# Layer 0 of a graph-then-attention kernel: two product reads placed between the left sums, and a fixed order for the opening

## The chip, the cores and the metric

The kernel runs on one core of one Trainium2 chip. The metric is the device time of one execution in microseconds (us); the figure for a kernel is the median of its runs. The core has a matrix engine (TensorE, "PE" in the profile; its weight loads are listed apart as "PEld"), a vector engine (VectorE, "DVE"), an activation engine (ScalarE, "ACT"), a general engine (GpSimd, "POOL"), and a queue that issues the transfers (SyncE, "SP"). SBUF is the memory beside the engines, and PSUM the small memory in banks into which TensorE writes. Each engine runs its own list of instructions in order, and waits on semaphores for what other engines produce.

## The reference: what is computed

There are 64 batch elements of 256 nodes with 512 features, and one graph over the 256 nodes. Layer 0 mixes along the graph, layer 1 is masked attention with 8 heads; each ends in a residual addition and a normalization over the features.

```python
a = adj.astype(x.dtype)
deg = a.sum(axis=1)
# layer 0
mi = x @ Wi.T                      # Wi, Wj: the two halves of W
mj = x @ Wj.T
x = layernorm(x + deg * (mi + b) + a @ mj)
# layer 1: q, k, v = x @ W.T + bias, softmax over the neighbours only
# ... (cut)
x = layernorm(x + attn_out @ Wo.T + bo)
```

## The kernel before: the parts concerned

The kernel handles the batch in 32 groups of two elements, b1 and b2. Every block product is done as seven products of half size instead of eight (a scheme of the Strassen-Winograd kind): the left operand is split into blocks A11, A12, A21, A22, of which sums S1 to S4 are formed, and the right operand (the weights) into blocks and sums B11, B21, B22, T1 to T4. VectorE forms the left sums. In layer 0 the left operand is the input multiplied by the graph. The input is split first into a rounded part `xhi` and a remainder `xlo`, and the graph product of both parts lands in a PSUM bank `pa` for each of four chunks of 128 features.

A tile that is drawn from `bank(...)` takes the next of three PSUM banks in rotation. It can be written only when all readers of the tile that had this bank before are done.

```python
ps_m = ctx.enter_context(tc.tile_pool(name="ps_m", bufs=3, space=PSUM))
def bank(name):
    return ps_m.tile([P, 512], F32, tag="mm", name=name)
def in_order(ins):                      # the scheduler keeps the program's order for these
    tc.keep_in_program_order(ins)
def anywhere(ins):                      # the scheduler may move these on their engine
    pass
# ... (cut)
for n, w, j in ((B11, wiT, 0), (T3, wiT, 1), (B22, wjT, 1), (B21, wjT, 0)):
    nc.sync.dma_start(out=w0[:, n], in_=...)
    if n == B11:
        nc.sync.dma_start(out=b_bc, in_=b0.to_broadcast([P, D]))
load_x(1)
# ... (cut)
for t in range(NT):                     # the graph, transposed
    pt = bank("pt_a")[:, :N]
    # ... transposes into pt
    nc.vector.tensor_copy(graph[:, t, edges(t)], pt)
    nc.scalar.copy(aT[:, t, :], pt)
# ... (cut)
def split_x(b):
    in_order(nc.scalar.copy(xhi[b], xh[b]))
    in_order(nc.gpsimd.tensor_tensor(xlo[b], xh[b], xhi[b].bitcast(F32), ALU.subtract))
    if b == 0:
        degree_bias()                   # two tensor_scalar of 128x512 on VectorE
    in_order(nc.gpsimd.tensor_tensor(xh[b], xh[b], degb, ALU.add))
# ... (cut)
def combine_left(f, order=anywhere):
    nc.vector.tensor_add(f["S1"], f["A21"], f["A22"])
    nc.vector.tensor_sub(f["S2"], f["S1"], f["A11"])
    order(nc.vector.tensor_sub(f["S3"], f["A11"], f["A21"]))
    nc.vector.tensor_sub(f["S4"], f["A12"], f["S2"])
def take_input(b, c, pa):               # the same for one chunk of layer 0, from PSUM
    nc.scalar.copy(xl[b][:, c]..., pa[:, :3 * P])
    _, a12, a22, a21 = (pa[:, m * P:(m + 1) * P] for m in range(4))
    f = xS[b]
    nc.vector.tensor_add(f["S1"][:, c], a21, f["A22"][:, c])
    nc.vector.tensor_sub(f["S3"][:, c], f["A11"][:, c], a21)
    nc.vector.tensor_sub(f["S2"][:, c], a22, f["S3"][:, c])
    nc.vector.tensor_sub(f["S4"][:, c], a12, f["S2"][:, c])
def first_inputs(b):                    # only for the first element
    pas = [score_banks("pa")[:, 0, :] if c < 2 else bank("pa") for c in range(NC)]
    for k, part in enumerate((xhi[b], xlo[b])):
        for c in range(NC):
            # ... graph products of chunk c into pas[c]
            if k == 1:
                take_input(b, c, pas[c])
```

The seven products of layer 0 run in the order below; the products 3, 6 and 7 accumulate onto the banks of 1, 4 and 5 ("x", "y", "z"), so those must have been read first.

```python
def l0_steps(b):
    def add_to(dst, src):
        nc.vector.tensor_add(dst, src, dst)
    # step1: A11*B11 -> x, copied to u1 by ScalarE; GpSimd adds u1 to three quarters of xh
    # step2: A22*T4 -> w      step3: A12*B21 onto x
    def step4():
        product("y", "S2", T2, True)
        add_to(place(0, 1), banks["y"])
    def step5():
        product("z", "S1", T1, True)
        add_to(place(1, 1), banks["z"])
    # step6: S3*T3 onto y, add_to, norm of row half 1
    # step7: S4*B22 onto z, add_to, norm of row half 0
```

The opening, before the loop, and the last slot of each turn of the loop, in which the second element's steps 4 to 7 (`rest`) are mixed with the output projection of the group before (`o`):

```python
split_x(0)
for n, m, k in ((T1, T3, B11), (T2, B22, T1), (T4, B21, T2)):
    in_order(nc.vector.tensor_sub(w0s[n], w0s[m], w0s[k]))       # 128x1024 each
first_inputs(0)
in_order(nc.vector.tensor_sub(w0s[T3], w0s[B22], w0s[T3]))
p, q = l0_steps(0), l0_steps(1)
run([p[0], p[2], p[1]])
split_x(1)
run(p[3:5])
bias_steps()
make_factors(wqT, "wq", raw_q)          # four 128x512 subtractions on VectorE
run(p[5:])
l0_inputs(1, 0, ...); l0_inputs(1, 1)   # graph stage of the second element
make_factors(wkT, "wk", raw_k)
# ... (cut)
run(q[:2]); h_transpose(0, 1, True); run(q[2:3]); h_transpose(0, 0, True)
check_graph()
run(q[3:])
# ... (cut), then in the loop over 31 groups:
    inverses = divide_at_once(g, w + 1)   # two reciprocals, two multiplications on VectorE
    o = o_steps(g)
    rest = work[SLOTS]                    # steps 4 to 7 of layer 0, element b2
    run(o[:1] + rest[:1] + o[1:2] + rest[1:2])
    combine_left(oS[g], in_order)
    end_values(inverses)
    run(rest[2:] + o[2:5] + work[SLOTS + 1] + o[5:6] + work[SLOTS + 2] + o[6:])
```

Of the kernel before, what the change touches and what calls it, by code (L numbers as in the profile page):

```python
# [225 lines left out]
def unshifted_path(ctx, tc, flag, x, adj, wiT, wjT, b0, wqT, bq, wkT, bk, wvT, bv, woT, bo, out):  # L226
# [70 lines left out]
    def load_x(b):  # L297
        if b < B:
            xh[b] = p6.tile([P, NT, D], F32, tag="xh", name="xh")
            nc.sync.dma_start(out=xh[b], in_=x[b].rearrange("(t p) d -> p t d", p=P))  # L300
# [4 lines left out]

    for n, w, j in ((B11, wiT, 0), (T3, wiT, 1), (B22, wjT, 1), (B21, wjT, 0)):
        nc.sync.dma_start(out=w0[:, n], in_=w.rearrange("(c p) o -> p c o", p=P)[:, :, j * H:(j + 1) * H])
        if n == B11:
            nc.sync.dma_start(out=b_bc, in_=b0.to_broadcast([P, D]))
    load_x(1)  # L310


    ident = const.tile([P, P], F32, name="ident")
# [21 lines left out]
    def diagonal(t):  # L335
        return slice(2 * t * P, (2 * t + 1) * P)

    def edges(t):
        return slice((1 - t) * P, (3 - t) * P)
# [3 lines left out]
    for t in range(NT):  # L343
        pt = bank("pt_a")[:, :N]
        for i in range(NT):
            transpose(pt[:, i * P:(i + 1) * P], a[:, i, t * P:(t + 1) * P], ident)

        nc.vector.tensor_copy(graph[:, t, edges(t)], pt)
        nc.scalar.copy(aT[:, t, :], pt)

    inexact = const.tile([P, 1], F32, name="inexact")

    def check_graph():


        exact = p1.tile([P, NT, 3 * P], F32, tag="oS", name="exact")
        for t in range(NT):
            nc.vector.tensor_copy(exact[:, t, edges(t)], aT[:, t, :])
            nc.vector.tensor_scalar(exact[:, t, diagonal(t)], ident, deg[:, t:t + 1], None, ALU.mult)
        nc.vector.tensor_tensor(exact, exact, graph.bitcast(F32), ALU.not_equal)  # L360
        nc.vector.tensor_reduce(inexact, exact.rearrange("p t n -> p (t n)"), AX.X, ALU.max)
        nc.vector.tensor_scalar(maskT, aT, 0.0, MASK, ALU.is_equal, ALU.mult)

    def degree_bias():
        for t in range(NT):
            in_order(nc.vector.tensor_scalar(degb[:, t, :], b_bc, deg[:, t:t + 1], None, ALU.mult))

    xhi, xlo, xl, xS, hT, hS, qT, kT, vv, aoT, oS = ({} for _ in range(11))

    def split_x(b):  # L370

        if b < B:
            xhi[b] = p1.tile([P, NT, D], F32R, tag="xhi", name="xhi")
            in_order(nc.scalar.copy(xhi[b], xh[b]))
            xlo[b] = p1.tile([P, NT, D], F32R, tag="xlo", name="xlo")
            in_order(nc.gpsimd.tensor_tensor(xlo[b], xh[b], xhi[b].bitcast(F32), ALU.subtract))
            if b == 0:
                degree_bias()
            in_order(nc.gpsimd.tensor_tensor(xh[b], xh[b], degb, ALU.add))


    def load_bias(b, name):
# [82 lines left out]
        order(nc.scalar.activation(shift, below, AF.Identity, scale=rstd))  # L465
        order(nc.scalar.activation(t, t, AF.Identity, bias=shift, scale=rstd))  # L466

    def norm(t):
        norm_apply(t, *norm_stats(t))

    def left_blocks(a11, a12, a21, a22, s):
        return {"A11": a11, "A12": a12, "A21": a21, "A22": a22,
                "S1": s[:, 0], "S2": s[:, 1], "S3": s[:, 2], "S4": s[:, 3]}

    def combine_left(f, order=anywhere):
        nc.vector.tensor_add(f["S1"], f["A21"], f["A22"])
        nc.vector.tensor_sub(f["S2"], f["S1"], f["A11"])
        order(nc.vector.tensor_sub(f["S3"], f["A11"], f["A21"]))
        nc.vector.tensor_sub(f["S4"], f["A12"], f["S2"])


    def input_tiles(b):
# [28 lines left out]
    def first_inputs(b):  # L511

        input_tiles(b)
        pas = [score_banks("pa")[:, 0, :] if c < 2 else bank("pa") for c in range(NC)]
        for k, part in enumerate((xhi[b], xlo[b])):
            for c in range(NC):
                for t in range(NT):
                    graph_product(b, c, pas[c], k * NT + t, t, part)
                if k == 1:
                    take_input(b, c, pas[c])  # L520

    def l0_steps(b):
        banks = {}

        def product(name, lname, n, first):
            if first:
                banks[name] = bank("po")[:, :H]
            for c in range(NC):
                matmul(banks[name], xS[b][lname][:, c, :], w0[:, n, c, :], start=(first and c == 0),
                                 stop=(c == NC - 1), skip_group_check=True)  # L530

        def place(t, j):
            return xh[b][:, t, j * H:(j + 1) * H]

        def add_to(dst, src):
            nc.vector.tensor_add(dst, src, dst)  # L536

        def step1():
            product("x", "A11", B11, True)
            u1 = p2.tile([P, H], F32, tag="lu", name="u1")  # L540
            nc.scalar.copy(u1, banks["x"])

            rest = xh[b].rearrange("p t (j o) -> p (t j) o", j=2)[:, 1:]
            nc.gpsimd.tensor_tensor(rest, rest, u1.unsqueeze(1).to_broadcast([P, 3, H]), ALU.add)  # L544

        def step2():
            product("w", "A22", T4, True)
            add_to(place(1, 0), banks["w"])

        def step3():  # L550
            product("x", "A12", B21, False)
            add_to(place(0, 0), banks["x"])

        def step4():
            product("y", "S2", T2, True)
            add_to(place(0, 1), banks["y"])

        def step5():
            product("z", "S1", T1, True)
            add_to(place(1, 1), banks["z"])  # L560

        def step6():
            product("y", "S3", T3, False)
            h = xh[b][:, 1, :].rearrange("p (j o) -> p j o", j=2)
            add_to(h, banks["y"].unsqueeze(1).to_broadcast([P, 2, H]))
            norm(xh[b][:, 1, :])

        def step7():
            product("z", "S4", B22, False)
            add_to(place(0, 1), banks["z"])  # L570
            norm(xh[b][:, 0, :])

        return [step1, step2, step3, step4, step5, step6, step7]

    def h_transpose(b, t, borrow=False):

        g, i = divmod(b, NB)
        if i == 0 and t == 1:
            hT[g] = p1.tile([P, NC, NB * N], F32, tag="hT", name="hT")
            hS[g] = pair_blocks(hT[g], "hS")  # L580
        pt = (score_banks("pt_h")[:, 0, :] if borrow else bank("pt_h")).rearrange("p (c n) -> p c n", c=NC)
        for c in range(NC):
            transpose(pt[:, c, :], xh[b][:, t, c * P:(c + 1) * P], ident)
        nc.scalar.copy(hT[g][:, :, i * N + t * P:i * N + (t + 1) * P], pt)
        if t == 0 and i == NB - 1:
            combine_left(hS[g])

    def add_output_bias(b):

# [289 lines left out]
    raw_q, raw_k = load_raw(wqT, "kT"), load_raw(wkT, "oS")  # L879
    load_x(2)  # L880
    raw_v, raw_o = load_raw(wvT, "v"), load_raw(woT, "aoT")
    split_x(0)
    w0s = [w0[:, n] for n in range(7)]
    for n, m, k in ((T1, T3, B11), (T2, B22, T1), (T4, B21, T2)):
        in_order(nc.vector.tensor_sub(w0s[n], w0s[m], w0s[k]))
    first_inputs(0)
    in_order(nc.vector.tensor_sub(w0s[T3], w0s[B22], w0s[T3]))
    p, q = l0_steps(0), l0_steps(1)
    run([p[0], p[2], p[1]])
    split_x(1)  # L890
    run(p[3:5])
    bias_steps()
    make_factors(wqT, "wq", raw_q)
    run(p[5:])
    l0_inputs(1, 0, (score_bank, score_bank))
    l0_inputs(1, 1)
    make_factors(wkT, "wk", raw_k)
    for _ in range(AHEAD):
        bring()
    run(q[:2])  # L900
    h_transpose(0, 1, True)
    run(q[2:3])
    h_transpose(0, 0, True)
    check_graph()
    run(q[3:])
    q = qk_steps(0, qT, "qT", bq_sb, bqd)
    run(q[:1])
    fold_value_bias(raw_o)
# [16 lines left out]
    for g in range(NG - 1):  # L925
        load_x(NB * (g + 2))
        load_x(NB * (g + 2) + 1)
        work = layer0(g + 1)
        run(work[0])
        for w in range(2, NB * NC, 2):  # L930
            values(g, w - 2)
            values(g, w - 1)
            multiply()
            divide_two(g, w - 1)
            later = [scores(g, w), scores(g, w + 1)]
            part = work[w // 2]
            n = 0 if w == NB * NC - 2 else 1
            run(later[:n] + part[:1] + later[n:] + part[1:])
        w = NB * NC - 2
        values(g, w)  # L940
        values(g, w + 1)
        multiply()
        inverses = divide_at_once(g, w + 1)
        o = o_steps(g)
        rest = work[SLOTS]
        run(o[:1] + rest[:1] + o[1:2] + rest[1:2])
        combine_left(oS[g], in_order)
        end_values(inverses)
        run(rest[2:] + o[2:5] + work[SLOTS + 1] + o[5:6] + work[SLOTS + 2] + o[6:])
        end = finish_steps(g)  # L950
        q = qk_steps(g + 1, qT, "qT", bq_sb, bqd)
        k = with_output_bias(g + 1, qk_steps(g + 1, kT, "kT", bk_sb, bkd))
        v = v_steps(g + 1)
        run(q[:5] + end[:1] + q[5:6] + end[1:2] + q[6:7] + end[2:3] + k[:1] + end[3:4] + k[1:] + end[4:] + v[:1])
        split_x(NB * (g + 2))
        run(v[1:5])
        run([scores(g + 1, 0), scores(g + 1, 1)])
        run(v[5:])
# [93 lines left out]
```

## Time and profile before

| what | value |
|---|---|
| time, median of 3 runs | 3214.55 us (3214.35 to 3217.09) |
| span of the profiled execution | 3213.5 us |
| TensorE busy | 3180.5 us (99%) |
| VectorE busy | 1892.0 us (59%) |
| GpSimd busy | 1505.4 us (47%) |
| ScalarE busy | 1111.8 us (35%) |
| mean TensorE clock granted | 0.998 |

The profile covers one execution. Times are counted from the start of the span. In a list of instructions in order of time, the columns are start, duration, engine, line of the kernel, operation, output<-inputs, shape and number of instructions that were merged into the row; in brackets stands how long the engine had been idle before it, and what released it. In a list of waits, the columns are who waited for whom, the microseconds in total, how often, and the longest. A matrix product of a 128x128 by a 128x256 fp32 block appears as two MATMUL records, so that one layer-0 product of four chunks is a row "x8". Ends of matrix products are modelled, so that short gaps of TensorE may hide in its busy time; the start times are the safer reading.

### The profile page before, as it was taken

Reading aid. Unit: us, or ns where it says so; the run is one execution under the profiler, and the core shown is the slowest. Engines: PE = TensorE matmul, PEld = TensorE weight load, DVE = VectorE, ACT = ScalarE, POOL = GpSimd, SP = SyncE. Lnnn points to the kernel's source line nnn. Section 1 sums busy time; section 2 is a strip of 40 time slices with the busy share of each in tenths; the row PEclk is TensorE's granted clock in tenths of the full one; section 3 lists DMA queues with packets and bytes.
Section 4 is the critical chain, followed back from the end, with each engine's and each line's share of the span. In section 5 each row is a group of like instructions: output and inputs, shape, how many; then the busy total and the mean of one; then the engine's idle time right before and its main releaser. Section 6 shows DMA issues by size and latency. Waiting matters only on the chain. (4 is left out here: it accounts for less than half of the span.)

```text
span 3213.5 us, 48157 instructions
## 1 busy us (share of the span) xinstructions
PE 3180.5 (99%) x17398; PEld 2625.5 (82%) x17398; DVE 1892.0 (59%) x3847; ACT 1111.8 (35%) x2146; POOL 1505.4 (47%) x1191
## 2 busy tenths in 40 slices
PE   7999999999999999999999999999999999999998
PEld 6888888888888888888888888888888888888885
DVE  6655566555566555655556655556555565555665
ACT  2333333333333333333333333333333333333333
POOL 3454444544445444455444454344544445444443
PEclk9999999999999999999999999999999999999999
DMA  6234432344323343223442234432344322334223
GB/s 236 73 109 125 122 92 77 105 119 123 111 66 95 121 123 119 74 88 112 123 124 89 75 106 122 122 106 69 99 119 124 115 70 90 117 122 121 81 70 93
DMA packets 257167, 340.89 MB, mean 106 GB/s; under 512 B 29856, under 2 KB 154272, under 8 KB 256928
## 3 DMA queue, kind: packets, MB, share of 16 engines
q1 hardware_dynamic: 256928, 337.76, 35.0%
q8 instruction: 142, 2.33, 0.3%
q14 instruction: 97, 0.79, 0.1%
HBM read 274.73 MB, written 37.75 MB: 97 GB/s over the span
## 5 line engine op out<-in xcount | busy, mean ns | idle before, releaser
L460 POOL TENSOR_TENSOR rstd<-ve,mhalf 128x1 f32<-128x1 f32 x256 | 140.5, 549 | 817.0 <-DVE below L458 816.4
L287 PE MATMUL po<-w,xS 128*128 128x256 f32 x2048 | 474.9, 383 | 4.4 <-DVE xh L536 0.5
L287 PE MATMUL st<-hS,factor 128*128 128x256 f32 x2048 | 452.8, 380 | 2.1 <-DVE u L642 2.1
L769 POOL TENSOR_TENSOR pk<-pe 128x512 f32<-128x512 f32 x256 | 322.0, 1273 | 277.0 <-ACT pe L766 277.0
L287 PEld LDWEIGHTS po<-w,xS 128*128 128x128 f32 x2048 | 385.4, 191 | 76.3 <-DVE xh L536 17.3
L287 PEld LDWEIGHTS st<-hS,factor 128*128 128x128 f32 x2048 | 390.2, 191 | 54.3 <-DVE u L642 2.5
L287 PE MATMUL po<-w,xl 128*128 128x256 f32 x1536 | 353.3, 383 | 8.1 <-DVE xS L498 7.2
L766 ACT ACTIVATE pe<-pe 128x1024 f32<-128x1024 f32 x256 | 270.3, 1057 | 249.0 <-DVE pe L762 249.0
L287 PE MATMUL st<-hT,factor 128*128 128x256 f32 x1536 | 342.3, 380 | 1.0 <-DVE qT L673 1.0
L642 DVE TENSOR_TENSOR u<-st,u 128x512 f32<-128x512 f32 x96 | 66.4, 691 | 468.5 <-PE st L287 461.6
L762 DVE TENSOR_TENSOR pe<-ps,maskT 128x1024 f32<-128x1024 f32 x256 | 297.1, 1201 | 67.6 <-PE ps L287 67.6
L287 PEld LDWEIGHTS po<-w,xl 128*128 128x128 f32 x1536 | 287.8, 191 | 53.9 <-issue 18.1
L536 DVE TENSOR_TENSOR xh<-po,xh 128x256 f32<-128x256 f32 (+1 forms) x384 | 170.3, 457 | 270.0 <-POOL xh L544 197.4
L287 PEld LDWEIGHTS st<-hT,factor 128*128 128x128 f32 x1536 | 292.5, 191 | 40.1 <-DVE qT L673 1.4
L287 PE MATMUL ps<-qT,kT 64*128 64x256 f32 x2048 | 256.6, 390 | 0.0
L287 PE MATMUL pav<-pe,v_sb 128*64 128x256 f32 x2048 | 250.2, 386 | 1.9 <-ACT pe L766 1.8
L287 PEld LDWEIGHTS ps<-qT,kT 64*128 64x128 f32 x2048 | 187.4, 187 | 67.8 <-issue 51.3
L287 PE MATMUL st<-factor,hS 128*128 128x256 f32 x1024 | 234.8, 383 | 0.0
L287 PE MATMUL st<-factor,oS 128*128 128x256 f32 x992 | 229.5, 380 | 0.0
L839 DVE RECIPROCAL rden<-den 128x256 f32<-128x256 f32 x96 | 168.7, 1757 | 92.4 <-PE den L287 88.7
L287 PEld LDWEIGHTS st<-factor,hS 128*128 128x128 f32 x1024 | 192.5, 190 | 34.8 <-issue 10.6
L465 ACT ACTIVATE shift<-below,rstd 128x1 f32<-128x1 f32 x256 | 75.4, 294 | 415.1 <-POOL rstd L460 409.6
(112 smaller groups left out, 5035.0 us busy)
## 6 DMA issues: line engine op xcount, KB each, us to landing
xh<-in_x_dram SPq DMA_DIRECT2D x64, 512.0 KB, 4.1
factor<-wq SPq DMA_DIRECT2D x128, 256.0 KB, 2.7
factor<-wk SPq DMA_DIRECT2D x128, 256.0 KB, 2.7
factor<-wv SPq DMA_DIRECT2D x128, 256.0 KB, 4.4
factor<-wo SPq DMA_DIRECT2D x124, 256.0 KB, 2.7
out_dram<-xh SPq DMA_DIRECT2D x62, 512.0 KB, 3.7
factor<-in_wqT_dram SPq DMA_DIRECT2D x96, 256.0 KB, 2.7
factor<-in_wkT_dram SPq DMA_DIRECT2D x96, 256.0 KB, 2.7
```

Source lines behind the costliest of these rows:

```text
L287: in_order(nc.tensor.matmul(*args, **kw))
L460: nc.gpsimd.tensor_tensor(rstd, ve, mhalf, ALU.pow)
L465: order(nc.scalar.activation(shift, below, AF.Identity, scale=rstd))
L536: nc.vector.tensor_add(dst, src, dst)
L642: nc.vector.tensor_add(new("u2"), bank["y"], k["u1"])
L762: nc.vector.tensor_add(pe.rearrange("p j t q -> p j (t q)"), ps.rearrange("p j t q -> p j (t q)"), maskT.rearrange("p t q -> p (t q)").uns ...
L766: in_order(nc.scalar.activation(flat, flat, AF.Exp, scale=QSCALE, accum_out=etot[:, NB * g + i, pr:pr + 1]))
L769: nc.gpsimd.tensor_tensor(pk, pe[:, :, 0, :], pe[:, :, 1, :], ALU.add)
L839: nc.vector.reciprocal(rden, den)
```

## The change

It has two parts.

In the loop: the reads of layer 0's fourth and fifth product (steps 4 and 5) are now kept in the program's order, and the left sums of the output projection are issued in two pieces: S1 before the fifth product's step, S2 to S4 behind it. VectorE therefore reads the fifth product between S1 and S2, where the scheduler had it behind S3.

In the opening, nearly every instruction is put in a fixed order. The broadcast of layer 0's bias is fetched behind the weights. ScalarE rounds the first element ahead of its copies of the graph. The first remainder is computed by VectorE instead of GpSimd. The left sums of the first element are formed kind by kind over all four chunks, from the last chunk to the first (S3 and S2, then the degree bias, then S1, then T3, then S4), three of the four PSUM banks are borrowed from other pools instead of two, the mask is made later, the bias of the second element is added later, and the first element's two norms stand behind the graph stage of the second. Both transposes of the first element come behind four products of the second.

```diff
     for n, w, j in ((B11, wiT, 0), ...):
         nc.sync.dma_start(out=w0[:, n], ...)
-        if n == B11:
-            nc.sync.dma_start(out=b_bc, in_=b0.to_broadcast([P, D]))
+    nc.sync.dma_start(out=b_bc, in_=b0.to_broadcast([P, D]))
     load_x(1)
+    round_x(0)                       # ScalarE, before the graph's transposes
 ...
-        nc.scalar.copy(aT[:, t, :], pt)
+        in_order(nc.scalar.copy(aT[:, t, :], pt))
 ...
-        pas = [score_banks("pa")[:, 0, :] if c < 2 else bank("pa") for c in range(NC)]
+        pas = [score_banks("pa")[:, 0, :], score_banks("pa")[:, 0, :],
+               ps_v.tile([P, 2, N], F32, tag="av", name="pa")..., bank("pa")]
         for k, part in enumerate((xhi[b], xlo[b])):
-            for c in range(NC):
+            for c in reversed(range(NC)):
                 ...
-                    take_input(b, c, pas[c])
+                    in_order(nc.scalar.copy(xl[b][:, c]..., pas[c][:, :3 * P]))
+        def sums(name):
+            for c in reversed(range(NC)):
+                if name == "S2":     # S3 = A11 - a21, S2 = a22 - S3
+                elif name == "S1":   # S1 = a21 + A22
+                else:                # S4 = a12 - S2
 ...
-        def add_to(dst, src):
-            nc.vector.tensor_add(dst, src, dst)
+        def add_to(dst, src, order=anywhere):
+            order(nc.vector.tensor_add(dst, src, dst))
 ...                                  # step4 and step5:
-            add_to(place(0, 1), banks["y"])
+            add_to(place(0, 1), banks["y"], in_order)
-            add_to(place(1, 1), banks["z"])
+            add_to(place(1, 1), banks["z"], in_order)
 ...
-    split_x(0)
+    remainder(0, nc.vector)
+    sums = first_inputs(0)
     ...                              # T1, T2, T4
-    first_inputs(0)
+    sums("S2"); degree_bias(); add_bias(0); sums("S1")
     ...                              # T3
+    sums("S4")
+    late = []
-    p, q = l0_steps(0), l0_steps(1)
+    p, q = l0_steps(0, late.append), l0_steps(1)
     run([p[0], p[2], p[1]])
-    split_x(1)
+    round_x(1)
+    remainder(1, nc.gpsimd)
     run(p[3:5])
+    add_bias(1)
     ...
     l0_inputs(1, 1)
+    for t in late:
+        norm(t, in_order)
     ...
-    run(q[:2])
+    run(q[:4])
     h_transpose(0, 1, True)
-    run(q[2:3])
     h_transpose(0, 0, True)
-    check_graph()
-    run(q[3:])
+    check_graph()                    # its instructions in order, the mask among them
+    run(q[4:])
 ...                                  # in the loop:
-        run(o[:1] + rest[:1] + o[1:2] + rest[1:2])
-        combine_left(oS[g], in_order)
+        left = left_steps(oS[g], in_order)
+        run(o[:1] + rest[:1] + o[1:2] + left[:1] + rest[1:2] + left[1:])
```

## The prediction

> **What bounds the kernel now.** I read the page's table of engines first: TensorE is busy almost all the time, so only what stops TensorE can be won. Then the waits of TensorE and of its weight loads, once for the first 160 us and once for the steady part from 160 to 3150 us; and last the two places in order of time.
>
> The page, part 1, on the engines:
>
> ```profile
> PE 3180.5 (99%) x17398; PEld 2625.5 (82%) x17398; DVE 1892.0 (59%) x3847; ACT 1111.8 (35%) x2146; POOL 1505.4 (47%) x1191
> ```
>
> That leaves 33.0 us of the span (3213.5 less 3180.5) in which TensorE is idle. The windows of 20 us show 18.6 us of it in the first 160 (160.0 less 141.4), the rest almost all in the end of the kernel, which the change doesn't touch. The waits of TensorE in the first 160 us:
>
> ```profile
> PE po L287 <- DVE xS L498: 7.2, 1, 7.2
> PE pt_a L290 <- DVE a L330: 4.2, 1, 4.2
> PE pa L287 <- ACT xhi L374: 2.2, 1, 2.2
> PE st L287 <- DVE u L642: 2.1, 1, 2.1
> ```
>
> One wait of 7.2 us for a left sum is the large one. The second is the fetch of the graph, which stays; the third the rounding by ScalarE; the fourth lies at 81 us and its cause isn't touched.
>
> In the steady part TensorE shows no idle time, but its weight loads do:
>
> ```profile
> PEld po L287 <- DVE xh L536: 15.8, 30, 0.5
> PEld po L287 <- DVE rden L839: 9.9, 30, 0.3
> ```
>
> The first comes once in each turn of the loop. The timeline of the first turn shows where:
>
> ```profile
> 142.60 1.89 PE L287 MATMUL st<-factor,aoT 128*128 128x256 f32 x8
> 142.97 2.36 POOL L704 TENSOR_TENSOR xh<-xh,u 128x1024 f32<-128x1024 f32 x1
> 143.79 2.08 DVE L476 TENSOR_TENSOR oS<-aoT 128x512 f32<-128x512 f32 x1
> 144.11 3.43 PEld L287 LDWEIGHTS po<-w,xS 128*128 128x128 f32 x16
> 144.33 5.74 PE L287 MATMUL po<-w,xS 128*128 128x256 f32 x24
> ...
> 147.60 0.41 DVE L536 TENSOR_TENSOR xh<-po,xh 128x256 f32<-128x256 f32 x1
> 147.94 0.68 DVE L479 TENSOR_TENSOR oS<-aoT,oS 128x512 f32<-128x512 f32 x1
> 148.06 1.59 PEld L287 LDWEIGHTS po<-w,xS 128*128 128x128 f32 x8 [0.53 <-DVE xh L536]
> ...
> 149.90 1.89 PE L287 MATMUL st<-factor,aoT 128*128 128x256 f32 x8
> ```
>
> The x24 are the fifth, sixth and seventh product of layer 0. The seventh adds onto the bank of the fifth, which VectorE reads only at 147.60 to 148.01, behind S1, S2 and S3 of the output projection. One product of eight takes 1.73 us from start to start (142.60 to 144.33), three should take 5.19, and they take 5.57 (144.33 to 149.90). So each turn loses 0.38 us that the busy time hides. The opening in order of time:
>
> ```profile
> 10.77 3.34 DVE L885 TENSOR_TENSOR w<-w 128x1024 f32<-128x1024 f32 x1 [0.27 <-DMA w<-in_wiT_dram]
> 14.28 1.85 POOL L544 TENSOR_TENSOR xh<-xh,u 128x768 f32<-128x768 f32 x1 [1.25 <-ACT u L541]
> 14.37 6.12 DVE L885 TENSOR_TENSOR w<-w 128x1024 f32<-128x1024 f32 x2
> 16.54 2.87 POOL L376 TENSOR_TENSOR xlo<-xh,xhi 128x1024 fp32r<-128x1024 f32 x1 [0.41 <-ACT xhi L374]
> ...
> 22.98 0.28 DVE L498 TENSOR_TENSOR xS<-pa,xS 128x128 f32<-128x128 f32 x1
> ...
> 23.40 3.75 PE L287 MATMUL po<-w,xl 128*128 128x256 f32 x8 [7.21 <-DVE xS L498]
> ...
> 23.70 1.22 DVE L887 TENSOR_TENSOR w<-w 128x1024 f32<-128x1024 f32 x1
> ```
>
> The three weight sums take 3.1 to 3.3 us each while GpSimd works, and the same operation takes 1.22 at 23.70, when GpSimd rests. They hold the left sums back to 20.41, and the product at 23.40 waits for S4 of chunk 2 (22.98 to 23.26), as its bank is the one that chunk's graph product had. It then runs slow: 3.55 us to the next product's start (26.95) instead of 1.73; the windows give a granted clock of 0.50 for 22 to 26 us.
>
> **What the Trainium skill says.** "SBUF — State Buffer", section "Who interferes with whom": a VectorE instruction with two SBUF inputs and a GpSimd instruction that reads SBUF exclude each other, one blocks until the other is done; a VectorE instruction with at most one SBUF input outside its two-port modes doesn't. The trace agrees: L885 at 10.77 ends 1.08 us behind the GpSimd addition that ends at 13.03, the next starts to work when L544 ends at 16.13, S1 at 143.79 ends 0.54 behind L704's end at 145.33; while the PSUM sums at 20.4 to 22.7 keep their 0.28 beside a GpSimd addition. "TensorE: Matmul & The Clock Gate", section "What's actually happening": the clock halves after an idle window of about 3.4 us and needs about as long a busy one to return. Here it was still 1.0 in 18 to 20 us and lower in 20 to 22, with TensorE idle from 16.2: between 3.8 and 5.8 us of idling; so the trace agrees roughly.
>
> **The loop, step by step.** In the changed order, VectorE runs: second reciprocal, second multiplication, read of the fourth product, read of the projection's third product (L697), S1, read of the fifth, S2, S3, S4. From the rows of the first turn: the second reciprocal ends at 143.09; multiplication 0.41 and read 0.36 take it to about 143.9; L697's product is done at 144.49, its read (0.68) ends near 145.2; S1 is blocked by L704 until 145.33 and ends near 145.95; the fifth product is done at 146.22 (144.33 plus 1.89), its read ends near 146.65. The seventh product's weights are wanted at 144.11 plus 2 times 1.73, 147.57. The slack is 0.9 us, so the wait goes. S4 ends near 148.5 instead of 148.62, and S2 is wanted only after 151. Nothing else becomes late. 31 turns by 0.38: 11.8 us less. The wait for the reciprocal (0.3 us, 30 times) lies in another slot and stays.
>
> **The opening, step by step** (estimates in us, from the rows of the kernel before). The input lands at 5.45 (issued 1.25, landing 4.2); ScalarE rounds it at once, 1.05, to 6.5 instead of 7.38: graph products from 6.55, 0.87 earlier. VectorE makes the remainder in 1.22, to 7.8, before it is wanted at 9.3. Graph products end near 11.0. As chunk 0 is now last and the first product begins with it, one ScalarE copy (0.48) lies open: first product from about 11.6 (before 11.84), third from 13.95 to 15.7. The bias (256 KB) behind the weights brings T3's, B22's and B21's landing forward by some 0.7, to about 10.0, 11.5 and 12.9 (before 10.7, 12.2, 13.6 by issue plus landing). GpSimd has nothing to do, so the three sums take 1.22 each: T4 is ready near 14.1 instead of 20.4. The second product then runs from 15.7 to 17.4, at full clock.
>
> The fourth product meets a new wait. The bank of chunk 3 now comes round to it (two graph banks, chunk 3, first, second, fourth product), so it needs S4 of chunk 3, which stands far back: S3 and S2 of four chunks to 16.15 (four pairs of about 0.51, as each S2 waits for its S3), degree bias 0.75 to 16.9, S1 0.8 to 17.7. Then T3, with two SBUF inputs, meets GpSimd's addition of the bias, which starts as the degree bias ends and takes 2.38, to 19.3; T3 ends at 20.4, S4 of chunk 3 at 20.7. So the fourth product starts near 20.8, instead of 26.95: TensorE idles 3.4 us there, less than the time after which the clock fell, but not by much.
>
> Four products by 1.73 take it to 27.7 (second element's graph stage; before 34.10, so 6.4 ahead). Behind it VectorE is the tighter engine: the four weight differences wait for GpSimd's second bias addition (to about 27.0) and end near 29.4, the read of the sixth product near 30.0, which holds the last graph chunk by some 0.3. The left sums of the second element (16, about 3.5 us) make its second product wait some 0.7, against 0.4 before. The first element's norms no longer lie ahead of them, and both transposes come behind four products, near 38.5, when the second norm is applied (near 38.4). The graph check of some 3.2 us stands ahead of the fifth product's read and makes the seventh wait about 0.65 (before 0.53). Layer 1's first product starts near 45.2 instead of 51.71: 6.5 us ahead. What follows (the waits at 54, 70 and 81 us) depends on the same chains and moves along.
>
> **Sum:** 11.8 and 6.5 make 18.3; 3214.55 less 18.3 is 3196.3. I take 3197, as some of the opening's small waits may be larger.
>
> **The rivals.** First: the loop's wait goes from the fifth product's read to something else. For it speaks that VectorE has the same work, and S1 stays blocked by GpSimd. Against it stand the 0.9 us of slack. If the read were still late, only the opening's 6.5 would remain: 3208. Second: the opening's new wait for chunk 3's S4 grows (degree bias late, GpSimd's addition winning twice) and crosses the time after which the clock halves; about 2 us at half clock and 2 more of waiting leave 2.5 of the 6.5: 3200. Third: the fetches bound the opening, since the DMA share is about 1.0 from 8 us on. If the weights don't land earlier, T4 is ready near 14.8, still before 15.7, so this costs nothing at first; only a landing 2 us later than I take would. Fourth, on the other side: T3 gets in ahead of GpSimd's addition, or VectorE's differences ahead of the second one; each would give 1 to 2 us more: 3194.
>
> **Range and chances.** The loop's share is the same number 31 times and I trust it to 1 or 2 us; if it fails, it fails nearly whole, which I give one chance in ten. The opening is a chain of estimates: 2.5 to 9. So 3191 to 3203 should hold it 8 times in 10. 2% is 64 us, while TensorE is idle 33 in all: faster by over 2% can't be reached; slower by over 2% would need 2 us per turn.
>
> **What would show it right or wrong.** In the changed kernel the weight loads' wait for the read of layer 0 (L563 there) should be gone from the steady part, and three products in the last slot take 5.2 us; a turn should fall from 99.08 (144.33 to 243.41, the same row a turn later) to 98.7. In the opening, the three weight sums should take near 1.2 each, the second product should follow the third without a gap, the fourth should wait for an S4 some 3 us, and the first layer-1 product should start near 45. I am wrong if a new wait of VectorE shows in the steady part, or if the granted clock falls again between 17 and 25.

## The result and the profile after

The changed kernel takes 3196.05 us (median of 6 runs, 3195.23 to 3197.2). The kernel before took 3214.45 us beside it (6 runs, 3213.8 to 3217.09). The ratio is 0.9941, with a 95% interval of 0.9928 to 0.9954: 18.4 us less, where the prediction's sum was 18.3.

The table of engines on the page after:

```profile
PE 3172.0 (99%) x17398; PEld 2621.1 (82%) x17398; DVE 1845.7 (58%) x3848; ACT 1109.4 (35%) x2146; POOL 1501.8 (47%) x1190
```

TensorE works 8.5 us less with the same 17398 instructions, and is idle 23.0 us (3195.0 less 3172.0) instead of 33.0. Of these 10.0 us, 6.0 lie in the first 160 us (18.6 to 12.6). Another 3.6 lie in the loop: in the kernel before, TensorE itself stood still for 0.12 us in nearly every turn ahead of the seventh product, gaps too short for the list of waits, and the prediction took the steady part to have no idle time. VectorE takes over one operation from GpSimd, the first remainder, and is still busy 46.3 us less, as it is blocked less: S1 in the first turn takes 0.68 us (below), and it took 2.08. The waits of TensorE in the first 160 us of the kernel after:

```profile
PE pt_a L290 <- DVE a L338: 4.1, 1, 4.1
PE po L287 <- DVE xS L534: 2.5, 1, 2.5
PE st L287 <- DVE u L670: 2.0, 1, 2.0
PE pa L287 <- ACT xhi L316: 1.0, 1, 1.0
```

The wait of 7.2 us for a left sum is now 2.5, and that for ScalarE's rounding has gone from 2.2 to 1.0. The first and third stay. The weight loads' waits in the steady part of the kernel after, those for layer 0's products ("po"):

```profile
PEld po L287 <- issue: 9.9, 30, 0.3
PEld po L287 <- DVE rden L867: 9.9, 30, 0.3
```

The line for VectorE's read of layer 0 (15.8 us in 30 turns before the change) is gone, and the wait for the reciprocal, of 0.3 us a turn, is the same as before. The last slot of the first turn in order of time:

```profile
136.71 2.35 POOL L732 TENSOR_TENSOR xh<-xh,u 128x1024 f32<-128x1024 f32 x1
...
138.06 5.34 PE L287 MATMUL po<-w,xS 128*128 128x256 f32 x24
...
138.94 0.68 DVE L485 TENSOR_TENSOR oS<-aoT 128x512 f32<-128x512 f32 x1
139.02 1.18 POOL L854 TENSOR_TENSOR rtot<-rtot,rden 128x256 f32<-128x256 f32 x1
139.99 0.42 DVE L563 TENSOR_TENSOR xh<-po,xh 128x256 f32<-128x256 f32 x1 [0.37 <-PE po L287]
140.33 0.68 DVE L486 TENSOR_TENSOR oS<-oS,aoT 128x512 f32<-128x512 f32 x1
...
143.24 1.89 PE L287 MATMUL st<-factor,aoT 128*128 128x256 f32 x8
```

The read of the fifth product (139.99) now stands between S1 (L485) and S2 (L486), ends at 140.41, and waits for TensorE itself rather than for VectorE's earlier work. Three products take 5.18 us (138.06 to 143.24) instead of 5.57. The opening in order of time:

```profile
8.86 1.23 DVE L914 TENSOR_TENSOR w<-w 128x1024 f32<-128x1024 f32 x1 [1.46 <-DMA w<-in_wiT_dram]
...
10.36 1.23 DVE L914 TENSOR_TENSOR w<-w 128x1024 f32<-128x1024 f32 x1 [0.28 <-DMA w<-in_wjT_dram]
...
11.89 1.22 DVE L914 TENSOR_TENSOR w<-w 128x1024 f32<-128x1024 f32 x1 [0.30 <-DMA w<-in_wjT_dram]
...
13.71 3.72 PE L287 MATMUL po<-w,xl 128*128 128x256 f32 x16 [0.46 <-ACT u L568]
...
16.13 2.35 POOL L382 TENSOR_TENSOR xh<-xh,degb 128x1024 f32<-128x1024 f32 x1 [14.42 <-DVE degb L374]
16.69 2.87 DVE L919 TENSOR_TENSOR w<-w 128x1024 f32<-128x1024 f32 x1
...
19.49 0.87 DVE L534 TENSOR_TENSOR xS<-pa,xS 128x128 f32<-128x128 f32 x4
...
19.91 7.14 PE L287 MATMUL po<-w,xS 128*128 128x256 f32 x32 [2.48 <-DVE xS L534]
```

The three weight sums take 1.2 us each, the second product follows the third without a gap (they are the x16 at 13.71), and the new wait is the one at 19.91: the fourth product waits for S4 of chunk 3 (the first of the four at 19.49), which stands behind T3 (L919). T3 takes 2.87 us instead of 1.2, since GpSimd's bias addition began 0.56 before it.

### The profile page after: what moved, and what is told of

The parts are those of the page before. It is cut to its first block, busy times and chain, and to the rows that moved or that the text cites. A ratio compares the mean times of both kernels' runs of the same rounds, so it can differ in the third digit from the quotient of the medians.

```text
span 3195.0 us, 48126 instructions
## 1 busy us (share of the span) xinstructions
PE 3172.0 (99%) x17398; PEld 2621.1 (82%) x17398; DVE 1845.7 (58%) x3848; ACT 1109.4 (35%) x2146; POOL 1501.8 (47%) x1190
## 5 line engine op out<-in xcount | busy, mean ns | idle before, releaser
L287 PE MATMUL po<-w,xS 128*128 128x256 f32 x2048 | 466.3, 381 | 2.5 <-DVE xS L534 2.5
L725 DVE TENSOR_TENSOR xh<-st,xh 128x512 f32<-128x512 f32 x186 | 144.9, 779 | 135.9 <-PE st L287 135.9
```

Source lines behind the costliest of these rows:

```text
L287: in_order(nc.tensor.matmul(*args, **kw))
```

## The experiments

The theory: the gain is the sum of two parts that don't touch each other, 0.38 us in each turn (the read) and some 6 us in the opening (GpSimd out of the way of the weight sums, and the second product off the bank of a late chunk). Rivals: the loop's wait has other causes than the read's place; the opening's gain comes from the fetches or the norms; or short waits bring TensorE's clock down, so that times move for another reason than the waits' length. Ratios are to the kernel before, run on the same chip beside the others.

**Each part alone.** The first kernel is the one before with the loop's part; the second the one after with the loop's part undone.

```diff
+        left = left_steps(oS[g], in_order)
-        run(o[:1] + rest[:1] + o[1:2] + rest[1:2])
-        combine_left(oS[g], in_order)
+        run(o[:1] + rest[:1] + o[1:2] + left[:1] + rest[1:2] + left[1:])
+   # reads of the loop's steps 4 and 5 in order; the opening untouched
```

> The loop's part alone, on the kernel before: fourth and fifth product's reads kept in order and S1 ahead of the fifth product's step, the opening as it was. Theory (the seventh product waits for the fifth's read, 0.38 us in each of 31 turns): 11.8 us less than before, about 3202.6; the first turn's three products in 5.2 us, the first layer-1 product still at 51.7. Rival (the gain is all in the opening, and a loop in which TensorE is always busy cannot give any): 3214.

> The opening's part alone: the changed kernel with the loop's reads and left sums as they were before. Theory: 6 to 7.5 us less than before, about 3208 (3207 to 3208.5); first turn's three products in 5.57 us again. With the loop's part alone the two savings should add up to the change's 18.4. Rival (all in the opening): 3196.

The loop's part alone: 3201.16 us (ratio 0.9961, 0.9947 to 0.9974) beside 3212.97, so 11.8 us less. The opening alone: 3207.06 us (0.9983, 0.9975 to 0.999), 5.9 less. Their sum of 17.7 is the whole change within the scatter. The first kernel's three products take 5.18 us (143.92 to 149.10), as expected:

```profile
143.92 5.34 PE L287 MATMUL po<-w,xS 128*128 128x256 f32 x24
149.10 1.89 PE L287 MATMUL st<-factor,aoT 128*128 128x256 f32 x8
```

One expectation failed: its first layer-1 product starts at 49.14 and not at 51.7, though its opening is that of the kernel before. The second and third weight sum take 3.97 us together there, and took 6.12. In that execution the second sum began 0.05 us ahead of a GpSimd operation (14.45 against 14.50) and GpSimd was held up (2.83 us instead of 1.85); in the other it began 0.09 behind it (14.37 against 14.28) and was held up itself. So the old opening, too, differs from one execution to the next.

With the loop's part undone, three products take 5.57 us again (139.26 to 144.83), and the wait is back in the steady part of the second kernel's profile (waits of the weight loads):

```profile
PEld po L287 <- DVE xh L569: 15.8, 30, 0.5
```

This kernel has the opening of the change, but its clock fell there:

```profile
19.63 8.83 PE L287 MATMUL po<-w,xS 128*128 128x256 f32 x32 [2.15 <-DVE xS L540]
```

The four products take 8.83 us instead of 7.14, behind a wait of 2.15 us that is shorter than the 2.48 of the change. The granted clock is half from 19.64 on, for 3.41 us. What decides this is worked out in the last section.

**What in the loop does it.** In the third kernel the read stands ahead of all four sums. In the fourth it stands behind all four, and S3 and S4 are formed twice (the same values, about 1.2 us of additional VectorE work) to make it later still.

```diff
-        run(o[:1] + rest[:1] + o[1:2] + left[:1] + rest[1:2] + left[1:])
+        run(o[:1] + rest[:1] + o[1:2] + rest[1:2] + left)              # third
+        run(o[:1] + rest[:1] + o[1:2] + left + left[2:] + rest[1:2])   # fourth
```

> The changed kernel, but all four left sums stand behind the fifth product's step, so that its read comes ahead of S1. Theory (only the place of that read matters, and S2 has over 3 us before it is wanted): the same time as the changed kernel, 3196 within 0.7, and no wait of the seventh product's weights. Rival (S1 must come first, or the sums come late and a product of the projection waits): 0.3 us a turn or more, 3205 and up.

> A dose of the suspected wait: the changed kernel with the fifth product's read behind all four left sums, and S3 and S4 formed a second time ahead of it (1.2 us more of VectorE in each turn, the same values). Theory: the read then ends about 1.7 us behind the moment when the seventh product's weights are wanted, so TensorE loses about 1.6 us in each of 31 turns: 3196 plus 49, 3245 (3240 to 3250). Rival (VectorE has slack, and a late read is caught up): 3196 to 3200.

The third: 3195.06 us (0.9942, 0.9929 to 0.9956), the change itself, with three products in 5.18 us (138.22 to 143.40) and no wait for the read; so it isn't important that S1 comes first. The fourth: 3301.92 us (1.0281, 1.0266 to 1.0295), 105.9 more than the change's 3196.05 and about twice the addition that I expected. Its last slot in the first turn, the lines that answer to those of the kernel after:

```profile
135.98 3.62 PE L287 MATMUL po<-w,xS 128*128 128x256 f32 x16
...
136.94 1.18 POOL L854 TENSOR_TENSOR rtot<-rtot,rden 128x256 f32<-128x256 f32 x1
137.57 1.10 DVE L486 TENSOR_TENSOR oS<-oS,aoT 128x512 f32<-128x512 f32 x1
...
141.00 1.21 DVE L563 TENSOR_TENSOR xh<-po,xh 128x256 f32<-128x256 f32 x2
141.47 1.59 PEld L287 LDWEIGHTS po<-w,xS 128*128 128x128 f32 x8 [2.28 <-DVE xh L563]
...
143.30 1.89 PE L287 MATMUL st<-factor,aoT 128*128 128x256 f32 x8
```

Three products take 7.32 us here (135.98 to 143.30), 2.14 more than in the change, by 31 turns 66 us. One thing I had not counted: with the read gone from between them, S2 meets GpSimd's addition of 136.94 and takes 1.10 instead of 0.68. The other 40 us are the clock. The mean granted clock of this execution is 0.987 against 0.999 in the change; the difference by 3300 us is 40. Two microseconds a line, the last column but two is the granted clock; the windows of the second turn:

```profile
240.00:242.00 2.00, 0.43 (x2) 0.02 (x1) 2.00 (x5) 0.00 (x0) 0.00 (x0) 1.00 0.00 0
242.00:244.00 2.00, 1.70 (x6) 1.37 (x7) 1.82 (x4) 0.00 (x0) 0.00 (x0) 0.75 0.00 0
244.00:246.00 2.00, 2.00 (x6) 1.62 (x5) 0.69 (x4) 1.11 (x2) 0.55 (x1) 0.50 0.00 0
246.00:248.00 2.00, 2.00 (x10) 1.69 (x10) 1.22 (x5) 0.29 (x1) 0.55 (x1) 0.90 0.00 0
```

TensorE idles for most of 240 to 242 and is back at 242.3. From 243.0 the clock is half: the column falls short of 1 by 0.25, 0.50 and 0.10 in three lines of 2 us, 1.7 us lost in a stretch of 3.41. The trace has 24 such stretches in 31 turns, and 24 by 1.7 are 41 us, the same sum. The five executions bear this out: 3298.0 us at a mean clock of 0.988, 3301.3 and 3301.9 at 0.987, 3307.3 and 3307.6 at 0.985, where 0.001 of 3300 us is 3.3. So the 2.1 us that a turn's three products took longer cost 105.9 by 31, 3.4 us.

**What in the opening does it.** Four kernels undo or shift one thing each. The fifth takes two borrowed banks, as before, so that the second product gets the bank of chunk 2 and waits for its S4. The seventh has the bias fetched behind the first weight block again, and the remainder made by GpSimd. The sixth is the seventh with the bias addition ahead of the weight sums, so that GpSimd works beside all three. The ninth applies the first element's norms where they were.

```diff
-        pas = [score_banks("pa")[:, 0, :], score_banks("pa")[:, 0, :], ps_v.tile(...)..., bank("pa")]
+        pas = [score_banks("pa")[:, 0, :] if c < 2 else bank("pa") for c in range(NC)]  # fifth
+        if n == B11:                                                         # seventh, sixth
+            nc.sync.dma_start(out=b_bc, in_=b0.to_broadcast([P, D]))
-    remainder(0, nc.vector)
+    remainder(0, nc.gpsimd)                                                  # seventh, sixth
+    degree_bias(); add_bias(0)           # sixth: here, ahead of T1, T2, T4
-    p, q = l0_steps(0, late.append), l0_steps(1)
+    p, q = l0_steps(0), l0_steps(1)                                          # ninth
```

> The changed kernel with the graph banks of the first element as before: chunks 2 and 3 from the three rotating banks, chunks 0 and 1 borrowed. Theory (a product waits for the left sum that reads its bank last): the second product now waits for S4 of chunk 2, so it starts near 20.0 us instead of 15.4, the fourth near 21.8 instead of 19.9; layer 1's first product comes 1.5 us later, and 1.7 more where the granted clock halves for one of its windows of 3.4 us in the longer gap. Rival (the banks don't matter, the weight sum T4 was what held the second product): no change, the second product at 15.4.

> The changed kernel with GpSimd's work where it was: remainder on GpSimd, bias fetched behind the first weights, and the degree bias and GpSimd's addition of it ahead of the three weight sums. Theory (VectorE's sums of two SBUF inputs and GpSimd's operations exclude each other): the three weight sums take more than 1.23 us each again, up to 3.3, T4 ends near 17.7 instead of 13.1, the fourth product starts near 23 to 24 instead of 19.9, and layer 1's first product 3 to 6 us later than 44.0. Rival (the weight sums wait for their fetches): 1.23 us each still, T4 by 14.

> The changed kernel with two small parts undone: the bias fetched behind the first weights, and the remainder on GpSimd. Theory: the remainder is ready before its graph products want it on either engine (8.6 against 8.9), so this costs nothing; the fetch delays the other three weight blocks by 0.7 us, and as VectorE's chain from T4 to the last left sum holds the fourth product, that starts 0.7 later, near 20.6, and layer 1's first product near 44.7. Rival (the remainder on VectorE is what freed the opening): the weight sums slow again and 3 us or more lost.

> The changed kernel with the first element's norms where they were, ahead of the second element's left sums. Theory: the two statistics (0.69 each) and six small operations on VectorE delay those sums by some 2 us, so the second element's second product waits 2 us longer; the transposes behind four products would not need the norms that early; layer 1's first product 1.5 to 2 us later than 44.0. Rival (VectorE has room there): no change at 44.0.

The kernel before took 3214.06 us beside these four (7 runs, 3211.48 to 3216.76).

| kernel | us, median and range (4 runs each, but for the change) | ratio, 95% interval | wait ahead of the fourth product (fifth kernel: the second) | first layer-1 product starts |
|---|---|---|---|---|
| the change (6 runs, beside another set) | 3196.05 (3195.23 to 3197.2) | 0.9941 (0.9928 to 0.9954) | 2.48 | 44.00 |
| fifth, two banks | 3197.79 (3197.23 to 3198.87) | 0.9951 (0.9934 to 0.9967) | 2.82 | 46.20 |
| seventh, old fetch and remainder | 3198.87 (3197.63 to 3200.61) | 0.9955 (0.9938 to 0.9972) | 3.68 | 46.52 |
| sixth, and GpSimd early | 3199.43 (3196.91 to 3200.89) | 0.9954 (0.9937 to 0.997) | 3.96 | 48.55 |
| ninth, norms early | 3199.07 (3197.47 to 3201.52) | 0.9952 (0.9936 to 0.9969) | 2.81 | 47.00 |

The intervals of these ratios overlap, so that the evidence is in the profiles and not in the medians. The fifth in order of time:

```profile
19.83 3.37 PE L287 MATMUL po<-w,xl 128*128 128x256 f32 x8 [2.82 <-DVE xS L533]
...
23.04 7.07 PE L287 MATMUL po<-w,xS 128*128 128x256 f32 x32
```

The banks do what was expected of them: the second product waits for a late S4 and starts at 19.83 (20.0 expected). It then takes 3.21 us to the next start (23.04) instead of 1.73, at half clock, so that the fourth product comes later than the 21.8 expected. The seventh in order of time:

```profile
6.10 2.37 POOL L380 TENSOR_TENSOR xlo<-xh,xhi 128x1024 fp32r<-128x1024 f32 x1 [4.39 <-ACT xhi L317]
10.83 1.23 DVE L915 TENSOR_TENSOR w<-w 128x1024 f32<-128x1024 f32 x1 [4.89 <-DMA w<-in_wiT_dram]
...
21.83 8.58 PE L287 MATMUL po<-w,xS 128*128 128x256 f32 x32 [3.68 <-DVE xS L535]
```

GpSimd's remainder is done at 8.47, before the graph products want it at 8.79, and the weight sums still take 1.23. So nothing that this profile shows comes from the remainder's engine; the first weight sum comes 2.0 us later (10.83 against 8.86) because its weights land later. I had expected 0.7. The fourth product starts 1.9 later, and its four products take 8.58 instead of 7.14, as the clock falls. The sixth in order of time:

```profile
10.09 2.36 POOL L383 TENSOR_TENSOR xh<-xh,degb 128x1024 f32<-128x1024 f32 x1 [1.54 <-DVE degb L375]
10.66 6.89 DVE L917 TENSOR_TENSOR w<-w 128x1024 f32<-128x1024 f32 x3 [0.71 <-DMA w<-in_wiT_dram]
```

With GpSimd beside them the three sums take 6.89 us instead of 3.7, T4 is ready at 17.55 instead of the seventh's 15.05, and layer 1 begins 2.0 us later than in the seventh. This is the mechanism that the kernel before suffered from, put back alone. In the medians it can't be seen (0.6 us, inside both ranges).

The ninth's expectation failed in its reason. Its first layer-1 product is 3.0 us later, but its four products at 20.37 take 10.17 us instead of 7.14: the clock is half for 6.83 us from 19.67 on. That begins well ahead of the first norm's statistics, at 31.07, so that the place of the norms isn't what brought it down. From the second element's first product to layer 1 it takes 13.79 us (33.21 to 47.00), the kernel after 13.93 (30.07 to 44.00). So the place of the norms by itself costs nothing that the profile shows; one profile doesn't say where the 3 us come from by which its median lies above the change's.

**Can the rest be had?** The new wait stands on T3, blocked by GpSimd. The eighth kernel forms the degree bias first, so that GpSimd's addition is done when T3 comes, and brings S4 ahead of S1 and T3. The tenth attacks the wait for "u" at 73 us: I put its lateness down to VectorE's four weight differences ahead of it, which are blocked by GpSimd adding the output bias; that addition is moved behind the products for the keys. The eleventh has both. A second run of the change stands beside them.

```diff
-    sums("S2"); degree_bias(); add_bias(0); sums("S1")
-    in_order(nc.vector.tensor_sub(w0s[T3], w0s[B22], w0s[T3]))
-    sums("S4")
+    degree_bias(); add_bias(0); sums("S2"); sums("S4"); sums("S1")     # eighth
+    in_order(nc.vector.tensor_sub(w0s[T3], w0s[B22], w0s[T3]))
-    k = with_output_bias(0, qk_steps(0, kT, "kT", bk_sb, bkd))
+    k = qk_steps(0, kT, "kT", bk_sb, bkd)                              # tenth
     run(k[:4]); make_factors(woT, "wo", raw_o); run(k[4:])
+    add_output_bias(0); add_output_bias(1)
```

> The changed kernel with the degree bias and GpSimd's addition ahead of all left sums of the first element (behind T4), then S3 and S2, S4, S1, T3. Theory (the fourth product waits for S4 of chunk 3 alone): that sum is done near 16.3 us, so the fourth product follows the second without the gap of 2.5 us; the fifth then waits about 1 us for the read of the first bank, which now stands behind T3. Layer 1's first product 1 to 2 us earlier, the whole 1.5 us less than the changed kernel. Rival (VectorE's later work is what sets the graph stage of the second element): the gap goes but nothing is gained behind 28 us.

> The changed kernel with the two GpSimd additions of the output bias to the first two elements moved behind layer 1's k steps, so that they no longer lie beside the four weight differences of Wo on VectorE. Theory (those differences have two SBUF inputs and are shut out while GpSimd adds 5.6 us): they take 0.7 each instead of up to 2.8, the wait of 2.0 us at 73 us goes, and with it the half clock that followed it in some executions: 2 to 3.7 us less than the changed kernel. Rival (the differences wait for their tile buffers, which transfers still read): the wait stays.

> The changed kernel itself once more, on the same chip as the three that follow, so that a microsecond or two can be told apart: 18 us below the kernel before, about 3196.

> Both together: the degree bias ahead, and the output bias later. If the two are independent, 3 to 5 us less than the changed kernel, about 3192; if the second only takes up the slack that the first makes, no more than the better of the two.

The change again: 3195.53 us (5 runs, 3194.5 to 3199.37; ratio 0.9948, 0.9934 to 0.9961). The eighth: 3193.03 us (3192.69 to 3193.37; 0.9937, 0.9923 to 0.9951), 2.5 less, and its five runs lie apart from all five of the change. In order of time:

```profile
12.74 0.88 DVE L374 TENSOR_SCALAR degb<-b_bc,deg 128x512 f32<-128x512 f32 x2
13.76 2.38 POOL L382 TENSOR_TENSOR xh<-xh,degb 128x1024 f32<-128x1024 f32 x1 [12.05 <-DMA bk<-in_bk_dram]
...
14.10 3.72 PE L287 MATMUL po<-w,xl 128*128 128x256 f32 x16 [0.46 <-ACT u L568]
...
17.66 7.30 PE L287 MATMUL po<-w,xS 128*128 128x256 f32 x32
```

The fourth product follows the second at 17.66 without a wait, and layer 1 begins at 41.78 (43.64 in the change run again). The wait of about 1 us that the fifth product was expected to have doesn't show: four products take 6.95 us (17.66 to 24.61), 1.74 each.

The tenth: 3195.26 us (3193.99 to 3195.83; 0.9943, 0.993 to 0.9957), no more than 0.3 below the change and inside its scatter. The expectation failed. The wait for "u" is gone, but this line is new among TensorE's waits of the tenth:

```profile
PE st L287 <- DVE kT L701: 1.0, 1, 1.0
```

and two of VectorE's rows in order of time are these:

```profile
72.66 0.69 DVE L426 TENSOR_TENSOR t<-raw 128x512 f32<-128x512 f32 x1 [1.62 <-DMA wo<-t]
74.13 0.88 DVE L701 SCALAR_TENSOR_TENSOR kT<-st,bkd,u 128x256 f32<-128x256 f32 x2 [0.79 <-PE st L287]
```

The third weight difference, now quick (0.69 instead of 2.83), waits 1.62 us for a buffer that a transfer still reads, as the rival had it. TensorE's new wait is for the read at 74.13, which had itself waited 0.79 us for TensorE's product; so the buffer's wait doesn't explain it, and why TensorE needs this read here and not in the change stays open. It waits 1.0 us a little later instead of 1.5. A transfer has a share in the wait for "u" of the change itself, too; in its first profile the read of "u" is 0.65 us behind one:

```profile
72.25 0.69 DVE L670 TENSOR_TENSOR u<-st,u 128x512 f32<-128x512 f32 x1 [0.65 <-DMA wo<-t]
```

The eleventh is the fastest: 3192.38 us (3192.21 to 3192.62; 0.9935, 0.9921 to 0.9948), 3.15 less than the change.

## Why the prediction was right

**The loop** went as written, nearly to the number. The read was expected to end 6.27 before 146.65, as the whole slot lies 6.27 earlier (144.33 to 138.06): at 140.38; it ended at 140.41. S1 came behind the projection's read and ended at 139.62, where 139.68 was to be expected; it took its ordinary 0.68 us, so that GpSimd's addition, which ended at 139.06, held it up by no time that shows. A turn took 98.69 us (138.06 to 236.75), where 98.7 was predicted. 31 turns by 0.39 are 12.1, and the loop's part alone gave 11.8. The third and fourth kernels show that the read's place is the cause. The first rival (the read still late) didn't occur. The line of the Trainium skill, "SBUF — State Buffer", section "Who interferes with whom", agrees with what the kernel after shows: T3 with two SBUF inputs was blocked (2.87 us), while the four S4, with one input in PSUM, took 0.87 us together beside GpSimd's next operation (18.56 to 21.24).

**The opening's steps.** The second column was predicted.

| step | predicted | measured |
|---|---|---|
| graph products start | 6.55 | 6.19 |
| first product, third product | 11.6, 13.95 | 11.26, 13.71 |
| T4 ready | 14.1 | 13.11 |
| fourth product starts, after a wait of | 20.8, 3.4 | 19.91, 2.48 |
| second element's graph stage | 27.7 | 26.70 |
| first layer-1 product | 45.2 | 44.00 |

The chain is there: the quick sums, the gap closed, the new wait for S4 of chunk 3 behind T3. One term was mis-sized, the fetch. The weights were taken to land 0.7 us earlier, in proportion to the 256 KB of the bias; the first weight sum started 1.9 earlier (8.86 instead of 10.77), and the seventh kernel, where the fetch order and the remainder's engine alone are undone, shows 2.0 and that GpSimd's remainder was in time. The third rival (weights that land no earlier) fell. The rest follows from that: with T4 ready 1.0 us early, the sums S3 and S2 were done at 15.19 instead of 16.15, T3 at 19.56 instead of 20.4, and the fourth product started 0.9 early.

**What was wrong: the clock, and "what follows moves along".** The prediction took a wait to be safe for the clock if it was shorter than the 3.8 to 5.8 us of idling after which it had seen the clock fall. Waits of 1.9 to 2.8 us brought it down in the kernels here. The second rival (the clock falls in the opening's new wait) did not occur in either profile of the change (waits of 2.48 and 1.83 us). It occurred in the second kernel, which has the same opening, behind 2.15 us, and so did the prediction's own sign of being wrong, a clock that falls between 17 and 25; it occurred also in the fifth, sixth, seventh and ninth, behind 2.8 to 4.0 us. That the first profile kept its full clock there was luck (last section), and a wait of the 3.4 us that was worked out would have needed more of it: the seventh's of 3.68 did bring the clock down.

Nor did the saving move along unchanged. Layer 1 began 7.7 us earlier in these two profiles (51.71 to 44.00), not 6.5. At the first products of layer 0 in the loop (a row of "po" from xl, at 106.00 before) the change was only 6.26 ahead, at 99.74. The windows of the kernel after, with the granted clock as the last column but two:

```profile
72.00:74.00 2.00, 1.01 (x5) 0.91 (x6) 0.69 (x1) 0.00 (x0) 0.00 (x0) 1.00 1.00 315
74.00:76.00 2.00, 2.00 (x6) 1.60 (x5) 0.13 (x1) 0.00 (x0) 0.00 (x0) 0.50 0.87 309
76.00:78.00 2.00, 2.00 (x7) 1.63 (x6) 1.25 (x2) 0.00 (x0) 1.27 (x1) 0.65 0.48 130
```

and the same stretch of the change run again:

```profile
74.00:76.00 2.00, 2.00 (x11) 1.74 (x11) 1.42 (x3) 0.00 (x0) 0.94 (x1) 1.00 0.97 300
```

After the wait of 2.0 us for "u", which ended at 72.99, the clock was half for 3.41 us from 74.00 in the first execution, and 1.7 us were lost. In the second the wait was 1.5 us, the clock stayed, and the loop's row stands at 97.25. So the total came out by two errors that cancel, the early fetch and the clock's loss, and its nearness to the number is in part luck. That row stands at 106.00 and 105.59 in the two profiles with the old opening, and at 97.25 to 100.93 in the five with the change's (the change twice, the second, third and fourth kernel), so that the opening is worth 4.7 to 8.8 us from one execution to another; the medians of the second kernel make it 5.9.

Taken from the first two profiles alone, 6.27 us ahead at the slot in the first turn and 31 by 0.39 make 18.4, the measured difference.

## What to carry to other kernels

A reader of a bank that is drawn again should be placed, in the engine's order, by when the next writer wants it and not by what was written first in the program: here a reordering that was worth 0.4 us a turn gave 12. Where two engines block each other, the order of their operations decides which of them pays: S1 went from 2.08 us to 0.68, and each weight sum from 2.8 to 3.3 us to 1.2, when they no longer met a GpSimd operation that had begun before them. Put waits of 1.9 us and more at the top of the list even where they look small, because each may bring a stretch of half clock after it, and look for the next wait that lies hidden behind the one you remove.

## What the runs showed of the hardware

- Short waits brought the clock down. The Trainium skill, "TensorE: Matmul & The Clock Gate", section "What's actually happening", has a free-running window of about 3.4 us, with half clock after at least one idle window. The window agrees: inside the kernels the stretches of half clock were 3.41 us long or twice that, and those of one trace start whole numbers of 3.413 us apart (in the fourth kernel at 242.98, 345.38, 447.78 and so on, thirty windows each). The condition doesn't: far less than a whole idle window was enough. Cut into these windows, the fourteen profiles show this: a full clock fell at the end of a window in which TensorE had been idle for 1.97 us or more in all 12 cases, with 1.87 to 1.95 us in 24 of 28, and with 1.83 or less in none. This is read from the traces afterwards; no kernel was made to try it.
- So it matters where a wait lies. The 2.48 us in the change's opening (17.43 to 19.91) lay across the edge of a window at 19.39, with 1.95 and 0.53 us in the two, and the clock stayed; the 2.15 us in the second kernel lay in one window, and it fell. In the fourth kernel the wait of 1.88 us lay inside one window in 26 of 31 turns, and the clock fell behind 24 of these. Each stretch costs 1.7 us, which accounts for much of the scatter: of the five executions of the change run again, 3194.5 to 3199.37 us, only the longest has a mean clock of 0.998, the others 0.999. The eleventh kernel, which has no wait above 1.2 us left in its opening but that for the graph's fetch, ran five times within 0.41 us.
- A broadcast of one bias row of 2 KB into 256 KB of SBUF held back the weights fetched after it. With the broadcast ahead of three weight blocks, the first weight sum starts at 10.66 to 10.83 us in four profiles; with it behind them, at 8.43 to 9.35 in the other ten, most often some 2 us earlier. At the pace of the weight blocks (512 KB every 1.5 us, as the sums at 8.86, 10.36 and 11.89 follow their landing) 256 KB would take 0.75 us; this is an estimate.
